# The FP4 layer of a fused network written as fixed lines, with its weights and first norms moved into the end of the convolution

## The chip, the cores and the metric

The kernel runs on one core of a Trainium2 chip. The core has engines that each run their own queue of instructions in order: TensorE (PE: matmuls and transposes, PEld: its weight loads), VectorE (DVE), ScalarE (ACT), GpSimd (POOL) and SyncE (SP, which issues most DMAs). They wait for one another through semaphores. SBUF holds working data as 128 partitions, PSUM takes the results of TensorE. The metric is the device time of one execution in microseconds (us); less is better.

## The reference

Four layers work on x, 8 sequences of 512 rows of 128 numbers in float32, each behind a layer norm and each added to its input. The change concerns the first two.

```python
x = x + _L0_attn_ref(_layernorm(x), ...)      # dynamic convolution over time
x = x + _L0_ffn_ref(_layernorm(x), w_gate, w_up, w_down)
x = x + _L1_attn_ref(_layernorm(x), ...)      # test-time training, "ttt"
x = x + _L1_ffn_ref(_layernorm(x), ...)       # mixture of experts
```

The convolution forms running means over time, from them 31 weights for each position and head (a softmax with a gate), sums the 31 weighted shifts, multiplies by `W_fc`, adds the layer's input and normalises again with `gamma` and `beta`. The second layer quantises everything that it multiplies, in blocks of 16 numbers:

```python
def fp4_quant_dequant(x):
    xb = x.reshape(shape[:-1] + (shape[-1] // BLOCK, BLOCK))
    scale = jnp.max(jnp.abs(xb), axis=-1, keepdims=True) / 6.0
    scale = jnp.maximum(scale, jnp.float32(1e-12))
    xn = xb / scale
    idx = jnp.searchsorted(_MID, jnp.abs(xn))
    q = _GRID[idx] * jnp.sign(xn) * scale
    return q.reshape(shape)
def fp4_linear(x, w):
    xq = fp4_quant_dequant(x)
    wq = fp4_quant_dequant(w)
    return jnp.einsum('bsk,nk->bsn', xq, wq)
gate = fp4_linear(x, w_gate)
y = fp4_linear(x, w_up)
h = jax.nn.silu(gate) * y
return fp4_linear(h, w_down)
```

`w_gate` and `w_up` are 352 x 128, `w_down` is 128 x 352.

## The kernel before

x stays in SBUF as 32 tiles of 128 rows. Four tiles are a group, and a group is a sequence, so the loops of both layers run over 0 to 7. Most of the program's order is set by a scheduler. Where it isn't, a `Line` chains each instruction of an engine to the one before it, so that the order of the source is kept on that engine.

**The convolution (`sequence_conv`, from L143)** is written with four lines (`vec`, `ten`, `act`, `gp`) and is pipelined by hand over sequences. For each sequence the running means are written to DRAM (`far<-avg`, L291) and read back in 8 DMAs as shifted windows, `base` (L294). The 31 taps are split into four groups of eight. The exponentials `en` are made for each group; for groups 0 to 2 ACT also writes the weights to PSUM (`w`, L362). `product(s, g)` (L411) multiplies windows and weights for one group on DVE. For groups 0 to 2 it does six of the eight numbers of a head (128x3072) with the weights from PSUM, and GpSimd does the other two from SBUF (`shared`, L402, each 128x512). For group 3 DVE does all eight (128x4096) from SBUF. PE sums the products in PSUM (`cv`, L420). DVE scales the sum (`cs`, L427), PE multiplies by `W_fc` and adds the residual (`pj`, L432 and L433; one buffer), DVE takes mean and variance, a reciprocal root follows by Newton steps, on GpSimd for sequences 0 to 6 (L130 to L138, L444, L445) and on DVE for sequence 7 (L85 to L93). ACT applies it (`v`, L451), and gamma and the sum into x follow on GpSimd (L455, L456), for sequence 7 on DVE. The part ends with sequence 6's finish, then sequence 7's scaling, projection, statistics, Newton and finish. The last thing it issues is zero fills in DRAM, on SP's queue (L1173, L1179).

**The FP4 layer (`fp4_ffn`, L627)** is left to the scheduler. `Norm` computes statistics (L569, L570), a Newton root (L85 to L93) and `off` (L576), here for groups 0 and 1 and later for 2 to 7. The weights are loaded into one tile, `wraw` (L649 to L654), in seven DMAs behind a GpSimd memset, quantised in two parts of 640 and 480 columns, transposed on PE (L665, L671) and copied to `w_in` and `w_out` by ACT. One call of `fp4` (L590) is nine instructions: DVE finds the largest of each block (L613), scales it (L614) and inverts it (L616); ACT multiplies that by a constant (`rc`, L617); GpSimd divides (`v`, L619); ACT writes the scaled magnitude to PSUM (`up`, L621, one buffer for all callers); DVE rounds in two instructions (L622, L623); GpSimd multiplies the scale back (L624).

A group runs `hidden`: ACT normalises (`xn`, L583), `fp4`, four transposes (L682) and a copy (`xt`, L684), and then for each of its four tiles two matmuls into `gu` (L692, two buffers), Silu on ACT (`sg`, L696) and the product on DVE (`h`, L697). Then `down`: `fp4` on h in two halves of 704 columns (`hq`), three sets of four transposes (`tp`, L708; two buffers, shared with `xt`'s and with `o`), copies (`ht`, L711), 16 matmuls that sum into `o` with x itself (L714, L716) and the copy back into x (L720). The loop calls `hidden(g + 1)` ahead of `down(g)`. The norm of the ttt layer that follows is spread in between by the scheduler. The ttt layer begins with `rows` (L799).

## Time and profile before

| | |
|---|---|
| time, median of 5 runs | 1305.17 us (1301.93 to 1306.41) |
| time of the profiled execution | 1303.8 us |
| its span, first to last instruction | 1302.1 us |
| mean granted TensorE clock | 0.945 |
| busy over the span: PE, DVE, ACT, POOL | 1102.3, 766.3, 493.9, 744.0 us |
| DMA | 67.26 MB, mean 52 GB/s |

The profile cuts the span into 40 slices of 32.6 us. The convolution takes the first eight of them (to about 255 us), the FP4 layer the next four (to 398.66 us), ttt goes on from there. The rows of these slices, in tenths of a slice:

```profile
PE   5899997457877699999988999999899785499992
DVE  6899999787984544444455444444547556123254
POOL 4357656545554688888822888888202444355553
PEclk9999999868998899999999999999999886699996
```

A digit of 9 means 90% or more. PEclk is the clock that the throttle granted to PE.

### The profile page before, as it was taken

The page shows a single profiled execution, that of the slowest core. Times are in us where ns is not written, and L with a number is a line of the kernel's source. Part 1 is how long each engine was busy: PE and PEld are TensorE (multiplying, and loading weights), DVE is VectorE, ACT ScalarE, POOL GpSimd, SP SyncE. Part 2 cuts the span into 40 slices and gives each one's busy share as a digit, 9 for nine tenths or more (in the row PEclk, how much of TensorE's full clock was granted, in tenths as well). Part 3 has the DMA queues.
Part 4 walks back from the last instruction along what each step waited for, and adds up shares of the span by engine and source line. Part 5 has one row for each costly group of instructions (what it writes and reads, how often), then busy time and mean ns, then how long its engine had stood idle before and what let it go on. Part 6 is the DMA issues. An engine that isn't in the chain of part 4 may idle for free.

```text
span 1302.1 us, 15373 instructions
## 1 busy us (share of the span) xinstructions
PE 1102.3 (85%) x5219; PEld 655.8 (50%) x5219; DVE 766.3 (59%) x1761; ACT 493.9 (38%) x1009; POOL 744.0 (57%) x724
## 2 busy tenths in 40 slices
PE   5899997457877699999988999999899785499992
PEld 2343432235655445555566455555675454277772
DVE  6899999787984544444455444444547556123254
ACT  4556545156556522222244222222433222133331
POOL 4357656545554688888822888888202444355553
PEclk9999999868998899999999999999999886699996
DMA  5224426760000000000000000000000100212267
GB/s 157 77 77 122 108 77 223 286 179 1 1 1 1 1 1 0 1 1 1 1 1 1 1 1 1 1 1 1 1 1 18 33 29 30 63 52 67 66 180 207
DMA packets 66894, 67.26 MB, mean 52 GB/s; under 512 B 6927, under 2 KB 48734, under 8 KB 66816
## 3 DMA queue, kind: packets, MB, share of 16 engines
q1 hardware_dynamic: 59296, 56.57, 14.7%
q0 software_dynamic: 4608, 8.43, 2.1%
q10 hardware_dynamic: 2912, 1.29, 0.4%
q8 instruction: 41, 0.67, 0.2%
q14 instruction: 37, 0.30, 0.1%
HBM read 40.00 MB, written 27.13 MB: 52 GB/s over the span
## 4 chain that ended last, share of the span: by engine, by line
PE 52%; DVE 10%; issue 5%; POOL 5%; ACT 5%; DMA 2%; another core or an unknown queue 1%; POOLq 0%; SPq 0%; DVEq 0%; ACTq 0%
PE ph L1135 5%; PE sum L1110 4%; PE pp L1125 4%; PE sum L1109 4%; PE sum L1111 4%; PE pa L1087 4%; PE ph L1429 4%; PE pb L1089 4%; PE po L1442 4%; PE pt L1118 2%; PE gu L692 2%; PE pa L906 1%; POOL v L619 1%; PE rows L799 1%
## 5 line engine op out<-in xcount | busy, mean ns | idle before, releaser
L1100 POOL TENSOR_TENSOR ds<-sw,s 128x512 f32<-128x512 f32 x64 | 81.7, 1276 | 86.9 <-DVE sw L1095 86.9
L1330 POOL DMA_INDIRECT rows<-xr,slot x64 | 62.6, 979 | 104.0 <-DVE rs L93 55.3
L1102 POOL TENSOR_TENSOR ds<-ds,s 128x512 f32<-128x512 f32 x64 | 111.3, 1739 | 5.0
L1093 ACT COPY b<-pb 128x512 f32<-128x512 f32 x64 | 37.5, 586 | 161.5 <-PE pb L1089 161.0
L1456 POOL DMA_INDIRECT res<-ye,xe x60 | 58.5, 974 | 66.6 <-DVE ye L1454 28.1
L1097 DVE TENSOR_TENSOR h<-sw,b 128x512 f32<-128x512 f32 x64 | 50.4, 787 | 70.6 <-ACT b L1093 70.3
L402 POOL TENSOR_TENSOR pr<-base,en 128x512 f32<-128x512 f32 x48 | 72.7, 1545 | 32.1 <-ACT en L364 32.1
L1432 ACT ACTIVATE ht<-ph,b 128x512 f32<-128x512 f32 (+2 forms) x100 | 55.8, 589 | 92.4 <-PE ph L1429 85.2
L1101 POOL TENSOR_TENSOR ds<-sw,ds 128x512 f32<-128x512 f32 x64 | 82.8, 1293 | 5.0
L1103 POOL TENSOR_TENSOR ds<-ds,b 128x512 f32<-128x512 f32 x64 | 81.5, 1273 | 5.0
L1125 PEld LDWEIGHTS pp<-proj,ht 128*128 128x128 f32 x512 | 67.1, 191 | 30.7 <-issue 29.3
L411 DVE TENSOR_TENSOR pr<-base,w 128x3072 f32<-128x3072 f32 x24 | 79.7, 3320 | 1.5 <-ACT w L362 1.5
L1442 PE MATMUL po<-w,ht 128*128 128x128 f32 (+1 forms) x640 | 77.4, 277 | 0.2 <-issue 0.2
L1120 ACT COPY ht<-pt 128x512 f32<-128x512 f32 x64 | 37.5, 586 | 102.1 <-PE pt L1118 102.1
L1095 DVE TENSOR_TENSOR sw<-pa,s 128x512 f32<-128x512 f32 x64 | 44.3, 692 | 54.2 <-ACT s L1091 54.2
L1429 PE MATMUL ph<-xt,w 128*128 128x512 f32 (+2 forms) x200 | 73.1, 509 | 2.7 <-DVE xt L1417 2.7
L1442 PEld LDWEIGHTS po<-w,ht 128*128 128x128 f32 (+1 forms) x640 | 73.9, 187 | 1.2 <-issue 0.4
L1137 DVE TENSOR_TENSOR db<-ph,sw 128x512 f32<-128x512 f32 x64 | 44.2, 691 | 47.1 <-PE ph L1135 47.1
L1135 PE MATMUL ph<-proj_t,dpt 128*128 128x512 f32 x128 | 71.6, 641 | 0.0
L420 PE MATMUL cv<-pr,sel 128*32 128x512 f32 x512 | 62.0, 611 | 11.2 <-DVE pr L411 10.7
L1087 PE MATMUL pa<-gate,kt 128*128 128x512 f32 x128 | 66.8, 604 | 2.5 <-ACT b L1093 2.4
L1110 PE MATMUL sum<-db,k 128*128 128x512 f32 x128 | 66.2, 598 | 1.6 <-DVE db L1137 1.6
(324 smaller groups left out, 2583.7 us busy)
## 6 DMA issues: line engine op xcount, KB each, us to landing
base<-far SPq DMA_DIRECT2D x64, 268.0 KB
rows<-empty SPq DMA_DIRECT2D x1, 5005.0 KB
res<-zero SPq DMA_DIRECT2D x1, 4096.0 KB
own<-zero SPq DMA_DIRECT2D x2, 2048.0 KB
w<-in_L_ffn_W SPq DMA_DIRECT2D x16, 256.0 KB
y<-res SPq DMA_DIRECT2D x16, 256.0 KB
xe<-rows SPq DMA_DIRECT2D x7, 585.0 KB
y<-own SPq DMA_DIRECT2D x12, 256.0 KB
```

The costliest lines, as they stand in the source:

```text
L402: gp(nc.gpsimd.tensor_tensor(pr[:, d, :], s["base"][:, d, at], s["en"][:, g, :], ALU.mult))
L411: vec(nc.vector.tensor_tensor(s["pr"][g][:, :nv, :], s["base"][:, :nv, at], w.to_broadcast([P, nv, L]), ALU.mult))
L1087: nc.tensor.matmul(pa, ki, gate, start=True, stop=True)
L1100: nc.gpsimd.tensor_tensor(ds, sw, s, ALU.mult)
L1101: nc.gpsimd.tensor_tensor(ds, sw, ds, ALU.subtract)
L1102: nc.gpsimd.tensor_tensor(ds, ds, s, ALU.add)
L1103: nc.gpsimd.tensor_tensor(ds, ds, b, ALU.mult)
L1110: nc.tensor.matmul(sums[1], ki, db, **kw)
L1125: nc.tensor.matmul(pp, ht[:, c * P : (c + 1) * P], proj[:, c, :], start=(c == 0), stop=(c == NF - 1))
L1135: nc.tensor.matmul(ph, dpt, proj_t, start=True, stop=True)
L1429: ten(nc.tensor.matmul(ph[:, :n], self.w1[:, e, c * P : (c + 1) * P], xt[:, :n], start=True, stop=True))
L1442: ten(nc.tensor.matmul(po[:m, i - lo, :], ht[:, c, (i - lo) * P : (i - lo) * P + m], self.w2[:, e, c, :], start=(c == 0), stop=(c == NF - ...
```

## The change

- `vec`, `ten`, `act` and `gp` become members of the context, so both layers share the four lines.
- For sequences 6 and 7 the weights of tap group 3 are also copied to PSUM, GpSimd does its two numbers of eight for that group too, and DVE's product there is 128x3072. Sequence 7's is cut in two pieces (128x2048 and 128x1024) with the sums of each behind it.
- A new class `Ffn` holds the FP4 layer's weights. They are loaded during sequence 5 into `tri`, a tile of the convolution that is dead by then, behind a memset on GpSimd.
- At the end of the convolution the weights are quantised in place, in three parts (384, 384, 352), by a new form of `Fp4` that shares its steps out. Sequence 6's finish now stands behind sequence 7's projection and behind the weights' division in the source. The table load for Silu comes here.
- Sequence 7's last norm and the first norm of the FP4 layer (groups 0 and 1) run through one Newton on DVE, with the rounding of the weights in between (`mix`). Sequence 7's gamma and sum are DVE instructions that take the mean and the root as scalars. ACT's `v` of sequence 7 is gone.
- `fp4_ffn` is rewritten as fixed lines, software-pipelined over three groups: the current one (`s`), the next two (`nxt`, `then`), the one whose norm is applied (`far`) and the one that is finished (`old`). The norm's Newton is split in groups 0 and 1, 2 and 3, 4 to 7. `up` of x takes a buffer of the transposes' pool, the buffers of `xn` become 3, of `sg` 4 and of `h` 2.
- The loads for ttt are issued behind the start of the first two groups. Only the norm of ttt is still spread by the scheduler in this layer.

```diff
-            product(cur, 3)
-            add_up(cur, 3)
-        finish(old, nc.gpsimd)
+            if b == B - 3:
+                ffn.load(flat(tri)[:, : ffn.NW], cur["spread"])
+            if b >= B - 2:
+                last_weights(cur)
+                shared(cur, NP, NGR)
...
+            if b < B - 1:
+                product(cur, 3)
+                add_up(cur, 3)
+        product(cur, 3, 0, NJ)
+        add_up(cur, 3, (0,))
+        product(cur, 3, NJ)
+        add_up(cur, 3, (1,))
...
+        q.greatest()
         scale_down(cur)
         project(cur)
-        norm1(cur, nc.vector)
-        finish(cur, nc.vector)
+        q.scales()
+        q.divide()
+        finish(old, nc.gpsimd)
+        act(nc.scalar.activation(warm, cx.eps[1e-5], AF.Silu))
+        q.addends([ps_w.tile([P, L], F32, tag=f"w{i}", name="up")[:, : hi - lo] for i, (lo, hi) in enumerate(q.parts)])
...
+        for _ in chain(norm.stats(0), norm.stats(1)):
+            pass
+        stats(pj, mv)
...
+        mix(norm.newton(0, 2, mv[:, :, 1]), chain(q.rounded(), centred()))
+        norm.offset(0, 2)
+        for j in range(G):
+            x = grp(cx.x, B - 1)[:, j, :]
+            vec(nc.vector.scalar_tensor_tensor(x, v[:, j, :], norm.all[:, j : j + 1], x, ALU.mult, ALU.add))
+        q.times(ffn.raw)
...
+        ffn.turned(turn)
+        for _ in chain(norm.stats(2), norm.stats(3)):
+            pass
```

The new helpers give these instructions in this order on each engine:

```python
def last_weights(s):
    w = ps_e.tile([P, L], F32, tag="e", name="w")
    act(nc.scalar.copy(w, s["en"][:, NP, :]))
    s["w"].append(w)
def mix(*steps):
    first, others = steps[0], list(steps[1:])
    for _ in first:            # one step of the first, then one of the others
        ...
```

The new loop over the groups, whole but for its guards at the ends (`if nxt`, `if old` and so on). `piece` is the reduction, scale, reciprocal, `rc` and division of half of h; `piece_up` and `piece_out` are its `up` and its last product; `inputs`, `inputs_up` and `inputs_out` are the same for x; `inputs_turn` is the transposes and the copy `xt`; `gated` is two matmuls into `gu` and the Silu; `turn` is four transposes and the copy `ht`.

```python
for g in range(NG):
    hidden(s, 0)
    gated(s, 2)
    hidden(s, 1)
    gated(s, 3)
    inputs_turn(nxt)
    piece(s, 0)
    hidden(s, 2)
    hidden(s, 3)
    piece_up(s, 0)
    piece(s, 1)
    turn(old, 0)
    turn(old, 1)
    all_of(s["q"][0].rounded())
    piece_out(s, 0)
    turn(old, 2)
    piece_up(s, 1)
    inputs(then)
    down(old)
    inputs_up(then)
    gated(nxt, 0)
    all_of(s["q"][1].rounded())
    piece_out(s, 1)
    if g == 0:
        all_of(norm.newton(4, NG))
        norm.offset(4, NG)
    normal(far, range(2))
    gated(nxt, 1)
    result(old)
    normal(far, range(2, G))
    all_of(then["x"].rounded())
    inputs_out(then)
```

Ahead of it stand, for the first two groups, their norms, `inputs`, the statistics of groups 4 to 7, the Newton of groups 2 and 3 and the first two `gated` of group 0. Behind it stand `turn`, `down` and `result` of the last group.

## The prediction

> **What bounds the kernel now.** I read the engine shares first (PE is 85% busy over the span, so only single stages can be decided elsewhere), then the chain of waits in 218 to 290 us, then the timeline of the convolution's end, of the layer's start and of one ordinary group. The diff ends where the ttt part begins, so all of it is priced up to the last copy of the layer's output, which ended at 398.66 us.

> The timeline of the convolution's end (start us, duration us, engine, line):

> ```profile
> 219.12 4.41 DVE L411 TENSOR_TENSOR pr<-base,en 128x4096 f32<-128x4096 f32 x1
> ...
> 220.76 7.63 POOL L402 TENSOR_TENSOR pr<-base,en 128x512 f32<-128x512 f32 x4 [2.03 <-ACT en L364]
> ...
> 223.45 3.34 DVE L411 TENSOR_TENSOR pr<-base,w 128x3072 f32<-128x3072 f32 x1
> ...
> 237.94 4.42 DVE L411 TENSOR_TENSOR pr<-base,en 128x4096 f32<-128x4096 f32 x1
> ...
> 238.09 4.33 POOL L135 TENSOR_TENSOR sq<-rs 128x4 f32<-128x4 f32 x1
> ...
> 242.41 1.92 PE L420 MATMUL cv<-pr,sel 128*32 128x512 f32 x16 [2.41 <-DVE pr L411]
> ...
> 243.92 1.50 ACT L451 ACTIVATE v<-pj,off,rs 128x128 f32<-128x128 f32 x4 [9.07 <-POOL off L445]
> ...
> 245.48 0.49 PE L432 MATMUL pj<-xn,ident 128*128 128x128 f32 x2 [1.14 <-ACT v L451]
> ```

> A product whose two inputs lie in SBUF holds GpSimd up: the four small products of L402 took 7.63 us beside the 4.41 us one, and one 128x4 operation took 4.33 us beside the other (its like took 0.20). With its weights in PSUM (128x3072) the product takes 3.34 us and nothing near it stretches. Sequence 7's projection waited for ACT's v of sequence 6, which waited for GpSimd's Newton steps.

> ```profile
> 247.57 0.89 DVE L255 BATCH_NORM_STATS2 s<-pj 128x6 f32<-128x128 f32 x4 [2.40 <-PE pj L433]
> ...
> 260.60 0.82 DVE L613 TENSOR_REDUCE sc<-wraw 128x40 f32<-128x640 f32 x1
> ...
> 261.73 1.26 ACT L583 ACTIVATE xn<-x,off,rs 128x128 f32<-128x128 f32 x3 [8.40 <-issue]
> ...
> 269.07 1.72 PE L665 MATMUL tp<-ident,wq 128*128 128x128 f32 x6 [21.54 <-POOL wq L624]
> ...
> 272.57 1.06 POOL L624 TENSOR_TENSOR xq<-v,sc 128x512 f32<-128x512 f32 x1 [2.30 <-DVE v L623]
> ...
> 274.83 0.59 ACT L684 COPY xt<-tp 128x512 f32<-128x512 f32 x1 [2.77 <-PE tp L682]
> ```

> From the projection's end (247.5) on, one chain runs: statistics, Newton, gamma, the norm of groups 0 and 1, then xn at 261.73. The weights are reduced only from 260.60, PE stands for 21.54 us, and the transposed first group (xt) is there at 274.83.

> ```profile
> 332.65 0.59 ACT L684 COPY xt<-tp 128x512 f32<-128x512 f32 x1
> ...
> 336.47 0.94 DVE L697 TENSOR_TENSOR h<-gu,sg 128x352 f32<-128x352 f32 x2
> ...
> 337.04 2.63 PE L692 MATMUL gu<-w_in,xt 128*128 128x352 f32 x8 [0.28 <-DVE h L697]
> ...
> 340.65 0.74 DVE L614 TENSOR_SCALAR sc<-sc 128x44 f32<-128x44 f32 x1
> ...
> 345.77 0.59 ACT L684 COPY xt<-tp 128x512 f32<-128x512 f32 x1
> ```

> In an ordinary group xt comes every 13.12 us (332.65 to 345.77). DVE is busy for 37.7 of the 40 us of 320 to 360, PE for 34.2. DVE is the bound, stalls like the 0.74 us of L614 (0.12 when free) among its busy time.

> ```profile
> 363.34 0.66 PE L708 MATMUL tp<-ident,hq 128*128 128x128 f32 x4 [1.24 <-POOL hq L624]
> ...
> 366.06 4.20 PE L692 MATMUL gu<-w_in,xt 128*128 128x352 f32 x8 [2.06 <-DVE h L697]
> ```

> Here PE idled 1.24 and 2.06 us in one group, and the next eight gu matmuls took 4.20 us, not 2.63.

> **The change, part by part.**

> 1. *Convolution's end.* Product (6,3) shrinks from 4.41 to 3.3 us, product (7,3) from 4.42 to 3.4 (2.2 + 1.2 in two pieces): 2.1 us, so DVE is through at 240.2, not 242.36. GpSimd takes two 128x512 products more for each of two sequences (2.5 us by L402's row of two at 230.92). For sequence 7 they fit into what L402's four lost above (7.63 against 5.22 us for sequence 6's four), and the Newton steps lose their 4.1 us stall; for sequence 6 a wait of 1.82 us covers most, and its offsets (218.73) are 5 us early. Uncovered, v of sequence 6 would be late by 2.5 us. The extra ACT copy to PSUM (0.59 us) lies in ACT's 2.86 us wait before 228.20.
> 2. *What eats most of that.* The projection has one PSUM buffer and still waits for v(6), and v(6) now stands on ACT behind the weights' rc. DVE needs for it: reduction of the weights 1.46 us (0.82 + 0.64, the two L613 rows on wraw), cs 0.69, scale 0.17, reciprocal 0.59, so 243.1; rc 0.24 and v 1.50 follow, PE projects 2.05 us: done at 246.9. That is 0.6 us earlier, not 2.1. The seven weight loads (573 KB) move on SP's queue to sequence 5, ahead of the last window loads: 3.1 us of issues (0.34 and twice 1.37) and 2 to 2.5 us at the 230 to 290 GB/s of that time. Those window loads end by about 212, and sequence 7's products start at 220.76, so 8 us cover them; uncovered, 3 us. The memset (0.74 us) lies in GpSimd's idle time.
> 3. *Joint Newton and weights.* From 246.9: statistics 1.2; then fifteen small steps and ten large ones interleaved. Six roundings of 384 or 352 columns by the 0.66 us of the 128x480 row are 3.2 us scaled, four 128x128 products with gamma 1.0, fifteen steps 0.13 to 0.20 each: 6.2 to 7.2 us, so the offsets are there at about 255. The weights run along: GpSimd's quotients (2.4 us by 1.28 for 640 columns), ACT's Silu table (1.28 us, moved from 277.33) and absolute values, products, nine transposes, three copies on ACT: last copy about 254.9. xn starts at 255.1, before 261.73: 6.6 us gained. Against it: Newton steps beside the three GpSimd products (2.4 us) can stall as L614 did; taken as 0, bound 2.4. On the other side 1.0 is to be had, if all fifteen steps cost 0.13. Behind v(6) on ACT stand the Silu table and the weights' absolute values, and behind v(6)'s products on GpSimd the weights' last ones, so the weights wait for the same thing.
> 4. *First group.* xn 1.6, reduction to rc 1.5, GpSimd 1.06, up 0.60, rounding 1.3, GpSimd 1.06, transposes at the half clock 1.12, xt 0.59 and hand-overs 0.8 give xt ready at 264.7. From the end of that rounding (about 261.8) DVE has the second group's scales (1.2), a Newton with sixteen statistics between (4.7), offsets and hand-overs (0.6) and a rounding (1.4) before the first h: 269.7, where it was 279.12. Gain 9.4.
> 5. *The loop as fixed lines.* DVE's work per group is the same; its order is now rigid, and one loop goes through all engines. From xt to the next xt: xt 0.48, rc 0.24, GpSimd v 1.39, up 0.69, second rc 0.13, ht 0.59, third transposes 0.48, down 3.83 (from o's rows at 341.19 to 345.02), eight gu 2.47, eight more 2.47, transposes 0.60 = 13.37, and eight hand-overs of 0.03 to 0.37 = 0.7: 14.1 us against 13.1. ht stands on ACT behind the second rc, and down, next group's gu and xt stand behind ht. Bounds: 13.1 (DVE's load, as now) and 15.2 (one stall of 1.1 on the loop, L614's longest row 1.22 less 0.12); I take 14.1, since every term is a row.
> 6. *Two Newton cycles.* Thirteen dependent steps of 0.21 us add 2.7 to two of the seven cycles; before, the first two cycles took 30.0 us (h 279.12 to 309.11) and the ttt norm's 16. Seven cycles: 5 x 14.1 + 2 x 16.8 = 104.1, plus 1 for cold gu's at the start (5.06 against 2.63 for eight, half of it on the path). Before: 279.12 to 379.71 = 100.6.
> 7. *Tail.* From the last group's first h to the end 19.0 before; all three transposes still follow one another, 19.5 after.

> **Sum.** 269.7 + 105.1 + 19.5 = 394.3 against 398.66: 4.4 us. The profiled execution took 1303.8 us (span 1302.1 and 1.7 around it), the median of five is 1305.17, 1.4 higher; the gain goes off the median: 1300.8.

> The row above (4.20 us) speaks of a clock that falls after two gaps close together. The loop of part 5 has one gap of 2.5 us in PE (from the second transposes to the third, while up, rc and ht pass) with single transposes ahead of it; the 2.41 us gap before the sums at 242.41 cost nothing (1.92 us for sixteen, 3.60 after the 4.61 us gap at 223.59). I take no loss, bound 1.6 us a cycle (4.20 - 2.63), 11 for seven.

> [...]

> **Rivals.**

> - *Gain kept in the convolution is halved (24%).* ACT runs in order, and xn stands behind the weights' copies. If GpSimd's three products or the Newton steps beside them stall (2.4 us), or v(6) comes later (2.5), the 4.4 shrink to about 1.9 or less: 1303 to 1307. For it: L135's 4.33 us and L614's 1.22. Against: the large roundings read PSUM, and L411 with PSUM weights stalls nobody. It is also the form in which the change would not do what it says: the weights off the path, but their wait back on it.
> - *Slower: PE's clock falls in the loop (26%).* Place: the gap before the third transposes; price 1.6 us a cycle. It takes the 4.4 us away after three cycles, decides against the kernel from five (8.0 - 4.4 = 3.6), and at seven gives 11.2 - 4.4 = 6.8: 1312. For it: the row at 366.06. Against: the row at 242.41.
> - *The loop is as short as before (4%).* If the gap between DVE's load and the fixed loop closes, 13.1 instead of 14.1 in seven cycles: 1294. Against it: every term of part 5 is measured.
> - *The forecast (46%)*: the sum, with part 3's 1.0 and loops down to 13.5 on one side (1295), some of the bounds used on the other: 1295 to 1302.6.

> A difference of 0.2% (2.6 us) is about what measurement can tell from none. Faster: 46 + 4 = 50%; within: 24%; slower: 26%. The range: down to the short loop's 4.4 + 7 = 11.4 off, 1293.8; up to 1310, six clock falls (9.6 - 4.4 = 5.2), leaving out only the seventh and its sum with part 3's bound.

> **What would show it.** Product 128x3072 at sequence 7's end near 3.3 us in two pieces, and no small GpSimd operation over 1 us there; projection over at 247; xn at 255; first h near 270; xt every 14.1 us, with ht starting right after the second rc; eight gu in 2.63 us in ordinary groups; last copy near 394. Wrong if gu take over 4 us in ordinary groups, if xt comes every 15 us or more, or if xn starts after 257.

## The result, and the profile after

| | before | after |
|---|---|---|
| time, median (58 and 34 runs side by side) | 1304.4 us (1301.69 to 1308.91) | 1303.66 us (1301.43 to 1310.68) |
| ratio, 95% interval | | 0.9999 (0.9992 to 1.0006) |
| span of the profiled execution | 1302.1 us | 1303.6 us |

No change can be measured. The time lies inside the range, but the range reached from 11 us faster to 5 us slower, so that says little; the likeliest case, 4.4 us faster, did not come. Rows of the slices of after, in tenths of a slice:

```profile
PE   5899997548777699999988999999899785499993
DVE  6899999888974444444455444444547556123255
POOL 3347756534544688888822888888202444355553
PEclk9899999868998999999999999999999987699997
```

The slices hardly differ: in the layer (ninth to twelfth) DVE is a tenth fuller in the tenth slice and a tenth emptier in the twelfth, PE a tenth fuller in the tenth and emptier in the ninth and eleventh. A mean over 32.6 us doesn't show where the time went; the timeline does. The profiled execution of after began 2.4 us late, in code that the change doesn't touch, so I count from the first thing that both kernels do alike at the convolution's end, the masking of sequence 7's last exponentials (`en<-en,mb`: 216.92 before, 219.29 after).

| us from there | before | after | forecast |
|---|---|---|---|
| last product of the convolution ends | 25.4 | 21.7 | 23.3 |
| projection of sequence 7 ends | 30.6 | 29.1 | 30.0 |
| first xn starts | 44.8 | 38.4 | 38.2 |
| first xt starts | 57.9 | 47.5 | 47.2 |
| first h starts | 62.2 | 52.1 | 52.8 |
| first h of the last group starts | 162.8 | 161.8 | 157.9 |
| last copy of the layer ends | 181.7 | 181.5 | 177.4 |

The layer's first h comes 10.1 us earlier than before, and from there to the last copy after takes 129.4 us where before took 119.5. The whole gain is given back inside the loop. The timeline of the convolution's end and of the first group in after:

```profile
234.31 6.65 DVE L423 TENSOR_TENSOR pr<-base,w 128x3072 f32<-128x3072 f32 x3
...
238.07 0.20 POOL L137 TENSOR_TENSOR sq<-rs 128x4 f32<-128x4 f32 x1
...
244.76 1.49 ACT L463 ACTIVATE v<-pj,off,rs 128x128 f32<-128x128 f32 x4
...
246.30 0.49 PE L444 MATMUL pj<-xn,ident 128*128 128x128 f32 x2 [3.29 <-ACT v L463]
...
257.69 3.19 ACT L657 ACTIVATE xn<-x,off,rs 128x128 f32<-128x128 f32 x8 [1.55 <-issue]
...
266.74 0.59 ACT L838 COPY xt<-tp 128x512 f32<-128x512 f32 x1 [0.52 <-PE tp L836]
```

The products of sequence 7's end are 128x3072 or pieces of it, the small GpSimd operation beside them takes 0.20 us where its like took 4.33, and the projection still waits for v of sequence 6. For xn's 1.55 us wait the profile names no releaser; it ends just behind the last sum into x on DVE (257.53). It costs nothing, since DVE has statistics until then and reduces xn only from 259.56. An ordinary group of after, PE's rows:

```profile
338.76 0.66 PE L873 MATMUL tp<-ident,hq 128*128 128x128 f32 x4 [0.24 <-ACT xt L838]
341.79 0.64 PE L873 MATMUL tp<-ident,hq 128*96 128x128 f32 x4 [2.37 <-ACT ht L874]
...
344.54 0.83 PE L882 MATMUL o<-w_out,ht 128*128 128x128 f32 x6
...
346.10 2.53 PE L843 MATMUL gu<-w_in,xt 128*128 128x352 f32 x8
```

This is the cycle of part 5, with its gap (2.37 us) before the third transposes and its eight gu in 2.5 us. But it does not look like this in every cycle. Two groups earlier the same instructions of the same kernel read:

```profile
309.94 0.66 PE L873 MATMUL tp<-ident,hq 128*128 128x128 f32 x4 [0.24 <-ACT xt L838]
312.97 1.05 PE L873 MATMUL tp<-ident,hq 128*96 128x128 f32 x4 [2.37 <-ACT ht L874]
...
314.25 1.49 PE L882 MATMUL o<-w_out,ht 128*128 128x128 f32 x6
```

1.05 for 0.64 and 1.49 for 0.83, behind the same 2.37 us gap. From first h to first h the seven cycles of after take 17.56, 16.68, 14.92, 13.90, 13.89, 16.79 and 15.94 us; the forecast had 17.8 for the first, 16.8 for the sixth (the ttt norm's Newton) and 14.1 for the others. So cycles 2, 3 and 7 are 2.6, 0.8 and 1.8 us too long, and the others right within 0.3. In each of those three TensorE's clock fell; cycle 2 besides begins at half the clock, after PE had stood 10.86 us in cycle 1, while DVE rounded and ran the Newton steps of groups 4 to 7 ahead of the next h:

```profile
289.51 4.14 PE L843 MATMUL gu<-w_in,xt 128*128 128x352 f32 x8 [10.86 <-DVE h L852]
```

The windows view of after shows it best if it is cut where the granted clock changes; the changes lie on a grid of 3.41 us (columns: window, its length, PE's busy time and instructions, granted clock, DMA share, GB/s):

```profile
289.17:292.58 3.41, 3.07 (x5) 0.50 0.02 5
292.58:296.00 3.42, 2.60 (x16) 1.00 0.00 0
296.00:299.41 3.41, 1.62 (x12) 1.00 0.00 0
299.41:302.82 3.41, 3.41 (x18) 0.50 0.01 2
...
306.24:309.65 3.41, 3.41 (x17) 1.00 0.00 0
309.65:313.06 3.41, 0.80 (x6) 1.00 0.01 2
313.06:316.48 3.42, 3.42 (x17) 0.50 0.00 0
...
336.96:340.37 3.41, 2.21 (x15) 1.00 0.00 0
340.37:343.78 3.41, 1.99 (x16) 1.00 0.00 0
343.78:347.20 3.42, 3.42 (x27) 1.00 0.02 5
...
371.09:374.50 3.41, 1.36 (x11) 1.00 0.00 0
374.50:377.92 3.42, 3.42 (x17) 0.50 0.02 5
```

The stay at 0.50 up to 292.58 is left from that wait (it began at 282.35, behind 278.93 to 282.34 at 1.00 with 0.00 us of PE work). Each of the three later windows at 0.50 follows one in which PE was busy for little of its 3.41 us: 1.62, 0.80 and 1.36. The gap in the window with 1.36 is the same one, before the third transposes, there 2.75 us long. In the ordinary group above the same gap (339.42 to 341.79) lies across an edge of the grid at 340.37, each side keeps about 2 us of work, and the clock stays. So in after the place of the gap on that grid went with the loss: one of 2.37 us left 0.80 us of work in its window and the clock fell, one as long left 2.21 and 1.99 in two windows and it did not.

### The profile page after: what moved, and what is told of

Its sections match the earlier page's. It is cut to its first block, busy times and chain, and to the rows that moved or that the text cites. A ratio compares the mean times of both kernels' runs of the same rounds, so it can differ in the third digit from the quotient of the medians.

```text
span 1303.6 us, 15342 instructions
## 1 busy us (share of the span) xinstructions
PE 1105.1 (85%) x5219; PEld 657.8 (50%) x5219; DVE 768.5 (59%) x1767; ACT 493.2 (38%) x1007; POOL 742.7 (57%) x730
## 4 chain that ended last, share of the span: by engine, by line
PE 62%; DVE 15%; ACT 10%; issue 5%; POOL 4%; DMA 2%; another core or an unknown queue 1%; SPq 0%; DVEq 0%; POOLq 0%; ACTq 0%
PE ph L1369 5%; PE sum L1344 4%; PE pp L1359 4%; PE sum L1343 4%; PE sum L1345 4%; PE pa L1321 4%; PE ph L1663 4%; PE pb L1323 4%; PE po L1676 4%; PE cv L432 3%; PE gu L843 2%; PE pt L1352 2%; DVE pr L423 2%; PE av L289 2%
## 5 line engine op out<-in xcount | busy, mean ns | idle before, releaser
L1327 ACT COPY b<-pb 128x512 f32<-128x512 f32 x64 | 37.5, 586 | 161.8 <-PE pb L1323 161.3
L412 POOL TENSOR_TENSOR pr<-base,en 128x512 f32<-128x512 f32 x52 | 75.8, 1490 | 31.8 <-ACT en L368 31.5
L423 DVE TENSOR_TENSOR pr<-base,w 128x3072 f32<-128x3072 f32 (+2 forms) x27 | 86.3, 3204 | 1.7 <-ACT w L366 1.7
L1335 POOL TENSOR_TENSOR ds<-sw,ds 128x512 f32<-128x512 f32 x64 | 82.8, 1294 | 5.0
L1337 POOL TENSOR_TENSOR ds<-ds,b 128x512 f32<-128x512 f32 x64 | 81.4, 1272 | 5.0
L432 PE MATMUL cv<-pr,sel 128*32 128x512 f32 x512 | 63.3, 626 | 6.2 <-DVE pr L423 5.8
```

The source lines that it names most:

```text
L423: vec(nc.vector.tensor_tensor(s["pr"][g][:, lo:hi, :], s["base"][:, lo:hi, at], w.to_broadcast([P, hi - lo, L]), ALU.mult))
L432: ten(nc.tensor.matmul(s["cv"][32 * j : 32 * (j + 1), :], sel[:, i].rearrange("p a h -> p (a h)"), s["pr"][g][:, i * NJ + j, :], start=(g ...
L1335: nc.gpsimd.tensor_tensor(ds, sw, ds, ALU.subtract)
L1337: nc.gpsimd.tensor_tensor(ds, ds, b, ALU.mult)
```

## The experiments

The runs came in three sets, each on one chip beside new runs of before. The chip of the first two sets took 1272 us for before; the kernel after took 1274.87 there, and from its first h to the last copy 129.43 us as on the first chip (129.44), so the layer can be compared over all runs. Below, "loop" is that stretch, and ratios are against before of the same set.

**Set 1: fill the gap, take the gap's cause away, or let the order go.**

`e1_fill`: six matmuls whose result is overwritten stand in the gap, so that PE has no idle time there.

```diff
+            for _ in range(6 if busy else 0):
+                ten(nc.tensor.matmul(tp[:, :FI], busy["xt"][:, :P], w_in[:, 0, :], start=True, stop=True))
...
-                turn(old, 1)
+                turn(old, 1, nxt)
```

> Six matmuls of 352 columns (6 x 0.31 = 1.9 us) are put on TensorE ahead of the second set of transposes of each group, into the tile that these then overwrite; they fill the 2.4 us in which TensorE stood there, and nothing else is changed. Theory A (the layer's loop is as summed, but TensorE's clock falls in that gap in three of seven cycles): granted clock 1.0 in all groups but the first, the cycles at 15.2, 14.9 and 15.9 us fall to 13.9, first h to last copy 129.4 -> about 125 us, time 1303.7 -> about 1299. Theory B (the fixed order alone costs the time, the clock is a by-play): the slow cycles stay within 0.5 us of what they were, time within 1.5 us.

Measured: 1278.94 us, ratio 1.0055 (1.0040 to 1.0070). The clock was 1.00 from 293 to 367 us and every ordinary cycle took 14.81 us. The size was wrong: a float32 matmul shows as two rows in the trace, so six are twelve, and they took 3.82 us where 2.37 were free. The run shows even cycles at full clock, but not what they are worth; `e1b_fill` repeats it with three.

`e2_turns`: the first two sets of transposes, with their copies on ACT, go ahead of `up` of the first half.

```diff
+            if old:
+                turn(old, 0)
+                turn(old, 1)
             piece_up(s, 0)
             piece(s, 1)
-            if old:
-                turn(old, 0)
-                turn(old, 1)
```

> The first two sets of transposes (and with them ACT's copies ht) stand ahead of the first half's up in the source, so that ACT makes them in the 1.5 us in which it waits for GpSimd. Theory C (the loop of part 5 of the prediction, through ht, third transposes and down, sets the ordinary cycle of 13.9 us): the cycle falls to about 13 us or less, time to 1294 to 1297. Theory D (the chain DVE h, gu, gu, x's transposes, xt, rc behind it on ACT, GpSimd, up, then all of DVE's roundings sets it, and the other loop only ties with it): ordinary cycles stay at 13.9 within 0.3; the clock falls less often and the last group's end is 2 us shorter, so time 1298 to 1301.

Measured: 1270.21 us, ratio 0.9982 (0.9966 to 0.9999). The ordinary cycle stayed at 13.88 us. So the chain of part 5 through ht and the third transposes is not alone in setting the cycle: with it shortened, something else of the same length holds it; that this is the chain through DVE is borne out by `e4b_loop`, not by this run. The loop took 126.4 us, since the clock was 1.00 from 291 to 358 us: the gap is now in two pieces, and the emptiest window up to 355 us had 1.83 us of PE work.

`e4_loop`: besides, the reciprocals of h and the scales of the next x come earlier on DVE and ACT (`piece(s, 0)` ahead of `inputs_turn(nxt)`, `inputs(then)` ahead of the first rounding), on top of the edit of `e2_turns`.

```diff
+            piece(s, 0)
             if nxt:
                 inputs_turn(nxt)
-            piece(s, 0)
...
+            if then:
+                inputs(then)
             all_of(s["q"][0].rounded())
             piece_out(s, 0)
...
             piece_up(s, 1)
-            if then:
-                inputs(then)
             if old:
                 down(old)
```

> As the run before, and besides rc and the division of the first half stand ahead of x's copy xt, and x's scales of the group after next ahead of the first half's rounding, where DVE waited 0.3 to 0.4 us for up and 0.4 for x's up. Theory D: ordinary cycle 12.9 us (13.9 less 0.5 for rc, less 0.5 for the waits), first h to last copy 129.4 -> about 119, time about 1293 to 1295. Theory C: no better than the run before. If neither holds and stalls of DVE's small operations beside GpSimd set the cycle (one of about 0.9 us a cycle, now in other places), it stays above 13.5.

Measured: 1276.91 us, ratio 1.0036 (1.0023 to 1.0049), cycles of 15.8 to 17.1 us in the third to sixth. Its timeline, DVE, ACT and PE:

```profile
325.65 1.25 DVE L722 TENSOR_SCALAR sc<-sc 128x32 f32<-128x32 f32 x1
...
327.33 0.23 ACT L727 ACTIVATE rc<-rc 128x32 f32<-128x32 f32 x1 [1.98 <-DVE rc L723]
327.46 0.56 ACT L874 COPY ht<-tp 96x512 f32<-96x512 f32 x1
...
328.08 0.49 PE L882 MATMUL o<-w_out,ht 96*128 96x128 f32 x2 [2.61 <-ACT ht L874]
```

My order put the third ht behind x's rc on ACT, and that rc behind a DVE scale stalled beside GpSimd (1.25 us). PE stood for 2.61 us in the middle of `down`; then the clock fell, once in each of these cycles (six of the following o matmuls took 1.46 to 1.49 us, where six at full clock take 0.83). The place of this one step cost 2 to 3 us a cycle against after; `e4b_loop` differs from `e4_loop` in nothing else.

`e5_free`: the same source and buffers, but no lines in the FP4 layer; the scheduler orders it.

```diff
+    cx.vec = cx.ten = cx.act = cx.gp = cx.ffn.norm.vec = cx.ffn.norm.act = lambda ins: ins
     vec, ten, act, ffn = cx.vec, cx.ten, cx.act, cx.ffn
```

> The FP4 layer's source stays as it is, but none of its instructions are chained in lines any more: the scheduler orders them as it did before the change. The convolution's end is unchanged. If the fixed order costs 0.8 us a cycle against the kernel before (13.9 against 13.1): ordinary cycles back near 13.1 and time about 1297 to 1300. If the cost lies in the split of the work (fewer buffers, up of x in the transposes' pool): ordinary cycles stay at 13.9 or above, time 1303 or more.

Measured: 1254.25 us, ratio 0.9853 (0.9838 to 0.9868), the fastest of all: 18 us under before, and far below both cases of the expectation. The loop took 106.5 us, its third to fifth cycles 11.8 to 12.5. The windows view of 300 to 360 us (window, length, then the busy time and instructions of PE, its weight loads, DVE, ACT and GpSimd, the clock, DMA share, GB/s), before, after and `e5_free`:

```profile
300.00:360.00 60.00, 50.16 (x293) 38.20 (x293) 52.58 (x120) 34.51 (x77) 32.23 (x26) 0.98 0.00 1
```
```profile
300.00:360.00 60.00, 49.02 (x280) 38.16 (x279) 52.07 (x114) 34.21 (x77) 31.27 (x26) 0.95 0.00 1
```
```profile
300.00:360.00 60.00, 55.40 (x331) 41.08 (x330) 57.51 (x129) 35.75 (x80) 36.06 (x29) 1.00 0.00 1
```

With the scheduler's order DVE is busy 57.5 of these 60 us, and the clock stays at 1.00 up to 367.30, in the last group. Between the second and the third transposes, where after's line makes PE wait 2.37 us, it now puts gu matmuls:

```profile
326.39 0.66 PE L874 MATMUL tp<-ident,hq 128*128 128x128 f32 x4 [0.27 <-ACT xt L839]
326.88 0.76 PE L844 MATMUL gu<-w_in,xt 128*128 128x352 f32 x2
327.48 0.60 PE L874 MATMUL tp<-ident,hq 128*96 128x128 f32 x4
```

**Set 2: the sizes again.**

`after_again`: the kernel after, unchanged.

> The changed kernel as it is, so that the runs of this set can be set against it on the same chip. Expected: within 0.2% of the kernel before, as in its own measurement (ratio 0.9999).

Measured: 1274.87 us, ratio 1.0016 (1.0007 to 1.0025), loop 129.43 us, clock windows as in after.

`e1b_fill`: three matmuls instead of six.

> As the first filling run, but three matmuls, not six: the trace of that run shows each float32 matmul as two passes, so six took 3.82 us and lengthened every cycle to 14.81 us, 0.9 more than the gap allowed, while no cycle was irregular any more. Three take 1.9 us and fit the 2.4 us gap. Theory A (clock): clock 1.0 and cycles of 13.9 us throughout (but for the two with a Newton), first h to last copy about 125 us, 4 to 5 us less than the changed kernel. Theory B (order alone): no gain, the long cycles stay.

Measured: 1272.31 us, ratio 1.0000 (0.9991 to 1.0009), 2.56 us under `after_again`; loop 126.96 us; cycles 17.63, 15.39, 13.88, 13.88, 13.89, 16.77, 15.77. It only adds work to PE (2.04 us in the gap) and is faster: that is the clock. Its windows where after fell twice, and its only later fall in the loop:

```profile
296.29:299.70 3.41, 2.86 (x20) 1.00 0.00 0
299.70:303.12 3.42, 3.42 (x29) 1.00 0.01 2
...
309.94:313.36 3.42, 2.87 (x19) 1.00 0.01 2
313.36:316.77 3.41, 3.41 (x28) 1.00 0.02 5
...
361.14:364.56 3.42, 1.02 (x4) 1.00 0.00 0
364.56:367.97 3.41, 3.41 (x9) 0.50 0.00 0
```

Both falls of cycles 2 and 3 are gone, which shortens these cycles by 1.3 and 1.0 us. Cycle 2 is still 1.5 us longer than the ordinary ones: that is its start at half the clock (its first eight gu took 4.17 us, those of cycle 3 2.63). In cycle 7 one fall takes the place of another. The fill keeps the window of after's fall busy, but now the clock falls earlier, behind the 3.15 us that PE stands for the Newton steps of the ttt norm (1.02 us of work in the window). The same wait in after, 3.16 us, lay across an edge of the grid, left a window 1.68 us of work and cost no clock.

`e4b_loop`: `e4_loop` with the order mended. The third transposes come before the next x's scales (the diff is against `e4_loop`).

```diff
             piece(s, 1)
+            if old:
+                turn(old, 2)
             if then:
                 inputs(then)
             all_of(s["q"][0].rounded())
             piece_out(s, 0)
-            if old:
-                turn(old, 2)
```

> The order of the earlier loop run, mended: there the third copy ht stood on ACT behind x's rc, which waited for DVE's scale (1.25 us, beside GpSimd), so that TensorE stood 2.6 us in the middle of down and its clock fell. Now the third transposes and their copy stand ahead of x's scales. If DVE's waits for up and for x's up (0.3 and 0.4 us) and the place of rc set the cycle: 12.9 to 13.3 us, first h to last copy about 120 us, time 7 to 9 us below the changed kernel. If the stalls of the small scale operations beside GpSimd (up to 1.25 us) grow by what the waits shrink, the cycle stays at 13.7 or above.

Measured: 1264.12 us, ratio 0.9935 (0.9921 to 0.9948), cycle 12.7 us, loop 120.7 us. With both chains shortened the cycle does shorten, below before's 13.1. So 14.1 was the price of this order, not of fixed lines as such.

`e9_free_oneup`: `e5_free`, but `up` of x goes back into the one PSUM buffer that all callers share, as before.

```diff
-s["x"].addends([ps_t.tile([P, W], F32, tag="t", name="up")])
+s["x"].addends([ps_u.tile([P, UP], F32, tag="up", name="up")[:, :W]])
```

> The layer without lines as in the run before (first h to last copy 106.5 us, cycles of 11.9), but x's up takes the same single PSUM buffer as h's up, as in the kernel before the change. If that buffer is what made the scheduler's order slow there (13.1 us a cycle): cycles of about 13, first h to last copy 114 to 118 us, about 10 us above the run without lines. If the gain of that run comes from the source's order and the split Newton: no more than 2 us above it.

Measured: 1267.1 us, ratio 0.9960 (0.9947 to 0.9974); loop 119.53 us, as long as before's (119.54), though not alike cycle by cycle. The own buffer for `up` of x, part of the change, is worth 13 us when the scheduler may use it. Part 5 passed over it because DVE's work "is the same".

**Set 3: the convolution's end by itself** (before 1304.8 us).

`e6_nolast`: without the PSUM weights and GpSimd's share in group 3 of sequences 6 and 7.

```diff
-            if b >= B - 2:
-                last_weights(cur)
-                shared(cur, NP, NGR)
```

> The changed kernel without its change to the last two sequences' products: no copy of tap group 3's weights to PSUM, DVE does all eight numbers from SBUF (128x4096, for sequence 7 in two halves). If part 1 of the prediction is right, its two products are 2.1 us longer together, GpSimd's Newton steps of sequence 6 stall again for some 4 us, and since the projection waits for ACT's v of sequence 6, xn starts 2 to 4 us later than in the changed kernel (38.4 us after the start of sequence 7's mask product, so 40.4 to 42.4); time 2 to 4 us above it. If the wait for the weights' rc sets the projection anyway, nothing moves (within 0.5 us).

Measured: 1311.04 us, ratio 1.0046 (1.0033 to 1.0058). xn starts 40.8 us after the masking, 2.4 later than in after, and two 128x4 operations on GpSimd take 2.12 us each again, one beside each 128x2048 product. The projection itself starts only 1.2 us later. Another 4 us were lost in the loop (133.4 us), which this edit leaves alone.

`e7_pj`: a PSUM buffer of its own for sequence 7's projection.

```diff
+            if s["b"] == B - 1:
+                s["pj"] = pj = ps_m.tile([P, G, D], F32, tag="m", name="pj")
...
-turn = [ps_m.tile([P, ffn.NK, P], F32, tag="m", name="tp")]
+turn = [ps_p.tile([P, ffn.NK, P], F32, tag="p", name="tp")]
```

> Sequence 7's projection gets a PSUM buffer of its own (the transposes of the weights take the other one), so that it need not wait for ACT's v of sequence 6. Part 2 of the prediction says that this wait costs: the projection then starts at cs's end, 2.3 us earlier. If it is on the path, xn starts 1.5 to 2.3 us earlier, and time falls by as much. If DVE's statistics of groups 0 and 1 and ACT's up of the weights, which wait for other things, set the joint Newton, xn moves by less than 0.7 us.

Measured: 1305.55 us, ratio 1.0000 (0.9988 to 1.0013). The projection no longer waits for v (it starts at 239.32) and xn starts 36.9 us after the masking, 1.5 earlier. In the profiled execution none of it reached the end, since the loop, again the same code, took 133.7 us. The clock accounts for this length and that of `e6_nolast`. Its windows in `e7_pj`, where the last cycles stay at half for two windows at a time:

```profile
357.84:361.25 3.41, 1.23 (x5) 1.00 0.00 0
361.25:364.66 3.41, 2.44 (x4) 0.50 0.00 0
364.66:368.08 3.42, 3.42 (x10) 0.50 0.00 0
...
371.49:374.90 3.41, 2.68 (x13) 0.50 0.00 0
374.90:378.32 3.42, 3.42 (x18) 0.50 0.02 5
```

PE work done at half the clock took twice as long here (eight gu 5.06 us there in before, from 275.47, and 2.53 at full clock in after), so by an estimate from these two, half of it is the most that it can cost. Summed over the windows at 0.50 that begin after the first h, for the four runs with the same loop:

| | PE work at half clock | loop |
|---|---|---|
| after | 13.3 us | 129.4 us |
| after_again | 13.4 us | 129.4 us |
| e6_nolast | 22.3 us | 133.4 us |
| e7_pj | 22.7 us | 133.7 us |

9.0 and 9.4 us more at half the clock should cost up to 4.5 and 4.7; the loops are 4.0 and 4.3 longer.

Executions of one kernel differ in the same way. Of the twelve of `e7_pj`, four had a mean granted clock of 0.945 to 0.948 and took 1300.56 to 1302.95 us; the eight others, among them the profiled one, had 0.941 to 0.944 and took 1305.29 to 1307.89. So the 1.5 us may reach the end where the clock holds; the median mixes both. Of the 36 executions of after, 28 had 0.945 to 0.949 (1301.43 to 1305.27 us) and eight 0.936 to 0.939 (1304.24 to 1310.68). Where in those eight the clock was lower is not on record.

`e8_free_pj`: the edits of `e5_free` and `e7_pj` together.

> Without lines in the layer, and with the projection's own buffer: the two that promise most together. The run without lines measured 0.9853 of the kernel before. Expected 0.984 to 0.986 if the projection's buffer brings 0 to 2 us; below 0.983 it would bring more than it does alone.

Measured: 1286.04 us, ratio 0.9854 (0.9839 to 0.9868), the same as `e5_free` has on its chip: the buffer adds nothing that can be measured.

`e11_freevec`: only DVE's line is taken out of the layer.

```diff
+    cx.vec = cx.ffn.norm.vec = lambda ins: ins
     vec, ten, act, ffn = cx.vec, cx.ten, cx.act, cx.ffn
```

> In the layer only DVE's line is taken away; TensorE, ACT and GpSimd keep the written order. If it is DVE's order that costs (it stood 4.3 us for Silu results and 2.8 us for up in 50 us), most of the 23 us between the fixed layer (129.4 us from first h to last copy) and the free one (106.5) comes back: under 115. If the orders of TensorE and ACT set the waits, DVE can only reorder within them: 122 us or more.

Measured: 1312.36 us, ratio 1.0065 (1.0052 to 1.0078), loop 137.0 us, ordinary cycles of 16.4 to 17.0. Freeing DVE alone does not help, so its fixed order is not what costs the 23 us by itself; the orders of PE, ACT and GpSimd take part. PE waited 15.2 us for ht in 300 to 360 us (3.8 at the longest); in after it was 9.5 us in 300 to 365 us (2.4). The clock fell in every cycle: 33.75 us of PE work lie at half the clock, against 13.3 in after, which could cost up to 10.2 us; the loop is 7.6 longer than after's.

## Why the forecast missed

- **Parts 1 to 4 were right in their totals, in part by luck.** Projection 29.1 (30.0), xn 38.4 (38.2), xt 47.5 (47.2), first h 52.1 (52.8). The last product came 1.6 us earlier than worked out, because the sums behind sequence 6's last product ran at full clock (1.92 us for sixteen from 224.88, at 1.00, instead of the 3.60 in before from 223.59, at 0.50). The projection came only 0.9 earlier: v of sequence 6 ends the wait, as part 2 said, and ahead of it DVE waited 0.95 us for PE's sums, which part 2 had left out. From there to xn it took 9.3 us, not 8.2: three Newton steps beside GpSimd's three products took 0.49, 0.52 and 0.63 us instead of 0.16, a stall of 1.2 us that part 3 took as 0. The two errors nearly cancel. `e6_nolast` confirms part 1's gain: without it xn is 2.4 us later.
- **Part 5's size was right, its reason only half.** The ordinary cycle is 13.9 us (14.1), but `e2_turns` shows that the chain through ht is not alone in setting it, and in `e4b_loop`, with both chains shortened, it is 12.7. The second chain was not shortened alone.
- **Parts 6 and 7 were right.** The Newton cycles take 17.6 and 16.8 us (17.8 and 16.8), the tail 19.8 (19.5).
- **The step that failed is "I take no loss, bound 1.6 us a cycle".** The choice of zero for seven cycles was wrong: in three of them the clock fell in the gap. Cycles 2, 3 and 7 are 5.2 us too long and the others gave 0.7 back: 4.6 us over the forecast's 105.1. Of the 5.2, 3.9 belong to these three falls (1.3, 0.8 and 1.8). `e1b_fill` shows the first two: without the falls these cycles are 1.3 and 1.0 us shorter. The third is read from the windows alone, since there that run only swapped one fall for another. The other 1.3 is the half clock with which cycle 2 begins, a fourth fall, behind PE's wait of 10.86 us, for which the prediction had no term. So the mechanism is the slower rival's, at the count at which it "takes the 4.4 us away": three cycles; its price of 1.6 us was too high for two of them.
- **The number matches another rival by chance.** 1303.66 lies in the band of the first one (1303 to 1307), which had the gain of the convolution halved. That did not happen: the first h came 10.1 us earlier, forecast 9.4, and the gain was lost behind it. The signs of being wrong spoke for the clock, too: the first eight gu of cycle 2 took 4.14 us, and one ordinary xt came after 15.2 us (294.12 to 309.30).
- **How I chose wrongly.** I weighed one gap that had cost nothing (2.41 us, before the sums) against one row that had slowed (366.06), as if a gap by its length either did it or not. The trace of before held the answer: its clock also stands at 0.50 in three windows of the loop (from 295.29, 298.71 and 366.97), the last behind a window with 1.34 us of PE work. Had I cut the windows there, seven cycles with 2.4 us gaps that drift over a 3.41 us grid would have suggested some falls, not none and not seven.
- **Not asked at all:** what the scheduler would do with the same source. The fixed order costs 23 us (129.4 against 106.5). The forecast compared two orders and called the bound DVE's load, though with an own buffer for x DVE can be busier (57.5 of 60 us in `e5_free`).
- **The late start of the profiled run** is no effect of the change. PE's first `eg` rows, with no difference in the code, in before and after:

```profile
18.93 1.96 PE L300 MATMUL eg<-avg,wbig 128*128 128x512 f32 x4 [0.77 <-ACT avg L288]
```
```profile
18.98 3.75 PE L304 MATMUL eg<-avg,wbig 128*128 128x512 f32 x4 [0.77 <-ACT avg L292]
```

The mask of sequence 7 starts either at 216.4 to 217.3 or at 219.0 to 219.5 us in the experiments too, whose code is the same up to there but in `e6_nolast`.

**Left open:** why the clock falls so often with a free order of DVE under fixed orders elsewhere was not taken apart further; nor was `e4b_loop`'s order tried with the gap of the last Newton cycle filled.

## What to carry to other kernels

Time won ahead of a hand-ordered loop can be lost in it again where PE has too little work in some window of 3.41 us (in this layer 1.73 us or less came before each fall of the clock): look at PE's busy time in windows of the clock's grid, not at gaps, and fill or split a gap that leaves a window with as little. Before fixing an order, build the same source and buffers without it: here that was 18 us faster than the kernel before, and the fixed order gave all of it back. Compare stages from a common instruction near them, since the same code can start 2 us later in another execution (the masking at 216.92 in before, at 219.29 in after).
